# The last residual of a mixture of experts: normed rows stored and fetched, or taken again from x with a diagonal

## The chip, the cores and the metric

The kernel runs on one core of one Trainium2 chip. The metric is the device time of one execution in microseconds (us), smaller is better. Work is done by TensorE (PE, with its weight loads shown apart as PEld), VectorE (DVE), ScalarE (ACT) and GpSimd (POOL); SyncE (SP) issues nearly all DMA transfers. Each engine works through its own instructions strictly in order, and an instruction that waits holds up what stands behind it on that engine. All data is float32.

## The reference

Four sub-layers follow one another on `x`, eight sequences of 512 tokens with 256 channels (as the kernel groups them): differential attention, a two-layer local attention network, a pair of diffusion attentions, and a mixture of experts. Each is applied as `x + layernorm(f(layernorm(x)))`. The change touches the last one:

```
def _ln(x, g, b):
    mu = jnp.mean(x, axis=-1, keepdims=True)
    var = jnp.mean(jnp.square(x - mu), axis=-1, keepdims=True)
    return (x - mu) * jax.lax.rsqrt(var + EPS) * g + b
...
gates = jax.nn.softmax(xf @ gate_w, axis=-1)
topw, topi = jax.lax.top_k(gates, K)
topw = topw / jnp.sum(topw, axis=-1, keepdims=True)
combine = jnp.sum(topw[:, :, None] * jax.nn.one_hot(topi, E, dtype=xf.dtype), axis=1)
h = jnp.einsum('td,edh->teh', xf, w1) + b1
h = _ln(h, ln1_g, ln1_b)
h = jax.nn.gelu(h, approximate=False)
y = jnp.einsum('teh,ehd->ted', h, w2) + b2
out = jnp.einsum('ted,te->td', y, combine)
out = _ln(out + xf, ln_g, ln_b)
...
x = x + _layernorm(_L1_ffn_ref(_layernorm(x, axis=-1), ...), axis=-1)
```

Here `xf` is the already normed `x`: `(x - mean) * rs`, with `rs` the inverse standard deviation of the row. There are 8 experts, each token goes to 2 of them. `out + xf` goes through a layer norm over the 256 channels, and that norm subtracts the mean of each row.

## The kernel before

`x` stays in SBUF for the whole kernel as 128 partitions by 32 tiles by 256 channels: `self.xb(b)` is sequence b, `NT` = 4 tiles of 128 tokens. The time runs through four stages; the mixture of experts is spread over three places.

**The gate** (`gate`, L1238 on). For each sequence, while the diffusion stage still runs for the next one, it takes the moments of the rows (`moments`, which returns `mv`, mean and variance, and `rs`), makes the normed rows `xf` on DVE (`normed`, L194), stores them to DRAM (L1248, one buffer `self.xf[b]` for each sequence, made in `scratch`), and goes on to the gate matmul, the choice of two experts and their places. `self.vals[b]` holds for each of the two choices and four tiles the place and the weight. GpSimd then scatters the rows to the experts' places in DRAM (L1311). The last sequence's gate has no diffusion work left beside it.

**The expert loop** (`experts`). The scattered rows come in 72 tiles of 128 (`load`, L1380). `hidden` turns a tile, multiplies it with the first weights and norms the result; in that stretch of the kernel `self.logs` is off, so `power` (L172, L173) makes `rs` on GpSimd, with an exponent of -0.5 read from `mhalf`. `outer`, three tiles later, turns, applies GELU on ACT, multiplies with the second weights and scatters the results to `self.got` (L1413). In between, by `between()`, the program records `weights(b)` for sequences 0 to 3: for each choice k and tile t a 128x128 diagonal matrix `dw[b][:, k, t]`, the identity times the token weights as a per-partition scalar, on GpSimd (L1457). A scheduler puts the instructions into each engine's order when the program is built; the trace shows where they ended up.

**The finish** (`finish`, `scaled`). For each sequence it loads the normed rows (`xfb`, L1419) and the two results of each token (`egot`, L1422), and PE adds them up in PSUM (`pz`): identity times the normed rows, plus the diagonal of each choice times its results. `scaled` norms them: bn_stats and bn_aggr on DVE (L184, L186), `rs` as a logarithm and an exponential on ACT (L169, L170, `self.logs` on), `nm` = -mean x rs on DVE (L1443), and the scaling itself on ACT into `ez` (L1445). Then DVE multiplies by the scale of the norm (L1429), GpSimd adds its bias (L1430), a second `scaled` norms `ez` in place, GpSimd adds `x` (L1434) and SP stores the sequence (L1435). The tiles of the pool `e_fin` (`xfb`, `egot`, `ez`) have two buffers each, `pz` six buffers of half a sequence, `edw` four. For sequences 4 to 7 the diagonals are made here, on ACT (L1459), each set when the buffer of four sequences before is free.

Of the kernel before, what the change touches and what calls it, by code (L numbers as in the profile page):

```python
# [9 lines left out]
F32 = mybir.dt.float32  # L10
BF16 = mybir.dt.bfloat16
AF = mybir.ActivationFunctionType
ALU = mybir.AluOpType
AX = mybir.AxisListType
PSUM = bass.MemoryType.PSUM

P = 128
NB = 8
NT = 4
S = P * NT  # L20
D = 256
# [99 lines left out]
class Net:  # L121
# [6 lines left out]
    def begin(self, ctx):  # L128
        nc = self.nc
        keep = ctx.enter_context(self.tc.tile_pool(name="keep", bufs=1))  # L130
        self.const = keep.tile([P, C_N], F32, name="const", tag="const")
        nc.sync.dma_start(self.const, self.a["const"])
        self.ident = self.const[:, C_ID:C_ID + P]
        self.mhalf = keep.tile([P, 64], F32, name="mhalf", tag="mhalf")
        nc.gpsimd.memset(self.mhalf, -0.5)
        self.x = keep.tile([P, NB * NT, D], F32, name="x", tag="x")

        signs = keep.tile([1, TH], F32, name="signs", tag="signs")
        with nc.allow_non_contiguous_dma(reason="scales"):
            nc.sync.dma_start(signs, self.a["L1_attn_tau_t"].rearrange("h i j -> (i j) h"))  # L140
        nc.vector.tensor_single_scalar(signs, signs, 0.0, ALU.is_ge)
        flag = keep.tile([1, 1], F32, name="flag", tag="flag")
        nc.vector.tensor_reduce(flag, signs, AX.X, ALU.min)
        self.flag = keep.tile([1, 1], mybir.dt.int32, name="iflag", tag="iflag")
        nc.vector.tensor_copy(self.flag, flag)
        self.load_rows(range(1))
# [390 lines left out]
    def local(self, nb, early, first):  # L537
# [3 lines left out]
        with ExitStack() as ctx:  # L541
# [242 lines left out]
            for b in range(min(2, nb)):  # L784
                begin(b)
# [4 lines left out]
            for c in range(total + 1):  # L790
                if c + 1 < total:
                    r.add(rotated(c + 1))
                elif c < total:
                    r.add(prepared())
                for u, calls in enumerate(slots):
                    if c < total:
                        scores(c, u)
                    if u == 2 and c:
                        g.add(gated(c - 1))
                    half = (len(calls) + 1) // 2  # L800
                    for f in calls[:half]:
                        f()
                    before = (c, u - 1) if u else (c - 1, 7)
                    if before in weights:
                        turned(*before)
                    for f in calls[half:]:
                        f()
                    if before[1] % 2 and (before[0], before[1] // 2) in sums:
                        attend(before[0], before[1] // 2)
                    if u in (2, 6) and c + 2 < nb:  # L810
                        save(c + 2) if u == 2 else begin(c + 2)
                qkv.pop(c - 1, None)
# [370 lines left out]
    def scratch(self, ctx):  # L1183

        nc = self.nc
        dram = ctx.enter_context(self.tc.tile_pool(name="rows", bufs=1, space=bass.MemoryType.DRAM))
        self.rows = dram.tile([ROWS, D + 1], F32, name="xrows", tag="xrows")
        self.got = dram.tile([2 * NB * S + TILES * P, D], F32, name="yrows", tag="yrows")  # L1190
        self.xf = [dram.tile([P, NT, D], F32, name=f"xf{b}", tag=f"xf{b}") for b in range(NB)]

    def clear_rows(self, ctx):
        nc = self.nc
# [29 lines left out]
    def load_routes(self, ctx):  # L1224

        w = ctx.enter_context(self.tc.tile_pool(name="routes", bufs=1))
        self.gatew = w.tile([P, DC, NE], F32, name="gate", tag="gate")
        self.nc.sync.dma_start(self.gatew, self.a["L1_ffn_gate_w"].rearrange("(c p) f -> p c f", p=P))
        self.routes = w
        self.slots = [w.tile([P, 2 * NT], mybir.dt.int32, name=f"slots{b}", tag=f"slots{b}") for b in range(NB)]  # L1230
        self.vals = [w.tile([P, 2, 2, NT], F32, name=f"val{b}", tag=f"val{b}") for b in range(NB)]
        self.runs = [w.tile([P, NT + 1, NE], F32, name=f"run{b}", tag=f"run{b}") for b in range(NB)]
        self.table_ = w.tile([P, 4, TILES], mybir.dt.int32, name="table", tag="table")

# [3 lines left out]
    def gate(self, b, wk, small, ps):  # L1238

        nc, tc, row = self.nc, self.tc, self.row_of  # L1240
        tie = row(C_TIE, NE * NE).rearrange("p (e f) -> p e f", f=NE)
        tiles = lambda x: [x[:, t, :] for t in range(NT)]
        made = self.moments(small, tiles(self.xb(b)))
        yield
        both = wk.tile([P, 2, NT, D + 1], F32, name="xf", tag="xf")
        xf = both[:, 0, :, 0:D]
        self.normed(tiles(self.xb(b)), tiles(xf), *made)
        nc.sync.dma_start(self.xf[b], xf)  # L1248
        for k in range(2):
            nc.gpsimd.tensor_scalar_add(both[:, k, :, D], row(C_TOK, NT), float((k * NB + b) * S))  # L1250
        yield
# [45 lines left out]
        two = small.tile([P, 2, 2, NT, NE], F32, name="two", tag="two", bufs=2)  # L1297
# [1 line left out]
            for i, x in enumerate((pos, p)):  # L1299
                nc.vector.scalar_tensor_tensor(two[:, i, k], rank, float(k), x, ALU.is_equal, ALU.mult)  # L1300
        val, slots = self.vals[b], self.slots[b]
        nc.vector.tensor_reduce(val, two, AX.X, ALU.add)
        nc.vector.tensor_copy(slots, val[:, 0].rearrange("p k t -> p (k t)"))
        den = small.tile([P, NT], F32, name="den", tag="den")
        nc.vector.tensor_add(den, val[:, 1, 0, :], val[:, 1, 1, :])
# [49 lines left out]
    def experts(self, nb, rest):  # L1355
# [5 lines left out]
        with ExitStack() as ctx:  # L1361
# [4 lines left out]
            nc, tc, g = self.nc, self.tc, self.ew  # L1366
# [48 lines left out]
                tc.add_to_no_dep_group("store", i.ins)  # L1415

            def finish(b):
                xf = fin.tile([P, NT, D], F32, name="xfb", tag="xfb")
                nc.sync.dma_start(xf, self.xf[b])  # L1419
                both = fin.tile([P, 2, NT, D], F32, name="egot", tag="egot")  # L1420
                for k in range(2):
                    nc.sync.dma_start(both[:, k], results[:, k, b])  # L1422

                z = fin.tile([P, NT, D], F32, name="ez", tag="ez")
                pz = [psf.tile([P, 2, D], F32, name="pz", tag="psf") for t in range(0, NT, 2)]
                for t in range(NT):
                    self.mm(pz[t // 2][:, t % 2], [(self.ident, xf[:, t, :])] + [(dw[b][:, k, t], both[:, k, t, :]) for k in range(2)])
                scaled([pz[t // 2][:, t % 2] for t in range(NT)], [z[:, t, :] for t in range(NT)])
                nc.vector.tensor_mul(z, z, g["lg"].unsqueeze(1).to_broadcast([P, NT, D]))  # L1429
                nc.gpsimd.tensor_add(z, z, g["lb"].unsqueeze(1).to_broadcast([P, NT, D]))  # L1430
                yield
                each = [z[:, t, :] for t in range(NT)]
                scaled(each, each)
                nc.gpsimd.tensor_add(z, z, self.xb(b))  # L1434
                nc.sync.dma_start(xout[:, b], z)  # L1435
                yield

            def scaled(srcs, outs):

                n = len(srcs)  # L1440
                mv, rs = self.moments(few, srcs)
                nm = few.tile([P, n], F32, name="nm", tag="fnm")
                nc.vector.scalar_tensor_tensor(nm, mv[:, :, 0], -1.0, rs, ALU.mult, ALU.mult)  # L1443
                for i, (x, o) in enumerate(zip(srcs, outs)):
                    nc.scalar.activation(o, x, AF.Identity, bias=nm[:, i:i + 1], scale=rs[:, i:i + 1])  # L1445

            fin, few = (ctx.enter_context(tc.tile_pool(name=k, bufs=b, side="right")) for k, b in (("e_fin", 2), ("e_few", 3)))
            dw = {}

            def weights(b):  # L1450

                dw[b] = few.tile([P, 2, NT, P], F32, name="edw", tag="edw", bufs=4)
                for k in range(2):
                    for t in range(NT):
                        w = self.vals[b][:, 1, k, t:t + 1]
                        if b < 4:
                            nc.gpsimd.tensor_scalar_mul(dw[b][:, k, t], self.ident, w)  # L1457
                        else:
                            nc.scalar.mul(dw[b][:, k, t], self.ident, w)  # L1459
                        yield  # L1460

            between = Between()
            for b in range(min(4, nb)):
                between.add(weights(b))
            loaded, made = {}, {}
# [15 lines left out]
            for b in range(nb + 1):  # L1481
                if b < nb:
                    parts[b] = finish(b)
                    next(parts[b])
                if b + 4 < nb:
                    between.add(weights(b + 4))
                    between.end()
                if b:
                    next(parts.pop(b - 1))
# [68 lines left out]
```

## Time and profile before

| what | value |
|---|---|
| runs of the kernel | 3848.53, 3854.63, 3860.05 us (median 3854.63) |
| the profiled execution | 3837.43 us, of which the span is 3835.7 us |
| PE busy | 3484.9 us (91%) |
| DVE, ACT, POOL busy | 2201.1 (57%), 1855.1 (48%), 1583.6 us (41%) |
| mean granted TensorE clock | 0.953 |
| stores of normed rows (L1248) | 8 of 512 KB, issued from 2792.1 to 3348.3 us |
| loads of normed rows (L1419) | 8 of 512 KB, the first two at 3423.9 us, the last at 3785.3 us |
| diagonals on POOL (L1457) | 32, median 593 ns, from 3372.8 us |
| diagonals on ACT (L1459) | 32, median 401 ns, 3752.9 to 3777.5 us |
| expert loop | first tile load issued at 3372.8 us, first `egot` load issued at 3742.8 us |
| finish | from there to the end of the span, 92.9 us |

In the timeline lines that follow, the columns are start and length in us, engine, line of the kernel, operation, the tile written and those read, the shapes and the count, and in brackets how long the engine was idle before and what released it. The windows view gives busy time, granted clock and DMA traffic for a stretch.

### The profile page before, as it was taken

What the parts mean: (1) busy time and instruction counts of PE and PEld (TensorE: products, weight loads), DVE (VectorE), ACT (ScalarE), POOL (GpSimd) and SP (SyncE); (2) the same over time, 40 slices, a digit from 0 to 9 for tenths busy, and PEclk for the clock granted to TensorE, in tenths of its full rate; (3) what the DMA queues carried; (4) which work ended last, traced back from release to release, by engine and by line L of the source; (5) the groups of instructions that cost most, each with busy time, mean ns of one, the idle gap of its engine ahead of it and who ended that gap; (6) DMA issues with size and microseconds to landing.
All of it is one profiled execution on the core that took longest, in us unless ns stands there. A gap on an engine that the chain in (4) does not pass through costs nothing. (4 is left out here: it accounts for less than half of the span.)

```text
span 3835.7 us, 53567 instructions
## 1 busy us (share of the span) xinstructions
PE 3484.9 (91%) x20034; PEld 1894.1 (49%) x20034; DVE 2201.1 (57%) x4364; ACT 1855.1 (48%) x3719; POOL 1583.6 (41%) x1432
## 2 busy tenths in 40 slices
PE   8999999999987999999999999997988889679985
PEld 3344444444434566665665555564444444446554
DVE  6777777677646666665555666663244443344445
ACT  3555555555543444444444444443655555223334
POOL 3666766676654433333333343321012211153334
PEclk8999999999979999999999999998999999789997
DMA  9300000000001000000010000000000000421115
GB/s 350 119 1 7 6 7 1 7 7 1 6 6 34 3 4 4 4 4 25 4 34 9 9 9 9 9 20 23 1 23 23 23 17 17 147 68 55 53 43 167
DMA packets 95138, 130.29 MB, mean 34 GB/s; under 512 B 24702, under 2 KB 73242, under 8 KB 94874
## 3 DMA queue, kind: packets, MB, share of 16 engines
q1 hardware_dynamic: 88346, 108.94, 8.8%
q0 software_dynamic: 6528, 17.87, 1.3%
q8 instruction: 162, 2.65, 0.3%
q14 instruction: 102, 0.84, 0.1%
HBM read 57.40 MB, written 65.18 MB: 32 GB/s over the span
## 5 line engine op out<-in xcount | busy, mean ns | idle before, releaser
L372 ACT ACTIVATE e<-sa 128x1024 f32<-128x1024 f32 (+3 forms) x512 | 359.4, 702 | 303.7 <-PE sa L365 299.3
L393 POOL TENSOR_TENSOR e<-e,e 128x1536 f32<-128x1536 f32 (+2 forms) x192 | 451.7, 2353 | 91.4 <-PE po L388 81.4
L365 PE MATMUL sa<-qT,kT 32*128 32x512 f32 (+3 forms) x2048 | 431.9, 498 | 9.2 <-ACT e L372 8.8
L369 DVE TENSOR_REDUCE spread<-sc 128x2 f32<-128x256 f32 (+3 forms) x512 | 422.2, 825 | 15.3
L355 PE MATMUL sc<-kT,qT 32*128 32x128 f32 (+3 forms) x2048 | 421.6, 493 | 7.9 <-DVE spread L369 4.5
L656 ACT ACTIVATE lp<-lp,lnm 128x256 f32<-128x256 f32 (+1 forms) x512 | 240.1, 470 | 260.4 <-DVE lnm L648 156.0
L660 POOL TENSOR_TENSOR lp<-lp,lrs 128x1024 f32<-128x1024 f32 x64 | 121.1, 1893 | 529.0 <-DVE lrs L657 508.9
L368 DVE TENSOR_TENSOR sc<-sc,const 128x256 f32<-128x256 f32 x512 | 218.6, 427 | 173.7 <-PE sa L365 140.7
L1088 ACT ACTIVATE te<-tsa 128x1024 f32<-128x1024 f32 x256 | 248.9, 1023 | 135.8 <-PE tsa L1084 88.7
L355 PEld LDWEIGHTS sc<-kT,qT 32*128 32x128 f32 x2048 | 160.7, 189 | 284.9 <-DVE spread L369 113.1
L213 PE MATMUL lpa<-ghT,lw 128*128 128x512 f32 x640 | 284.8, 600 | 12.1 <-ACT ghT L569 12.1
L213 PE MATMUL lqk<-qkv,lhT 128*128 128x512 f32 x512 | 247.7, 622 | 2.3 <-DVE qk L607 1.6
L608 POOL TENSOR_TENSOR qk<-qk,over 128x1024 f32<-128x1024 f32 x64 | 151.4, 2366 | 207.8 <-DVE qk L607 207.8
L375 POOL TENSOR_SCALAR_AFFINE_SELECT e<-e 128x512 f32<-128x512 f32 x256 | 160.5, 640 | 177.0 <-ACT e L372 176.6
L1407 ACT ACTIVATE ehT<-eht,enorm 128x128 f32<-128x128 f32 x288 | 108.3, 457 | 208.6 <-PE eht L1403 207.7
L213 PEld LDWEIGHTS lpa<-ghT,lw 128*128 128x128 f32 x640 | 119.3, 190 | 163.3 <-issue 136.3
L388 PE MATMUL po<-e,v 128*32 128x512 f32 (+3 forms) x2048 | 188.3, 451 | 4.0 <-POOL e L375 3.6
L365 PEld LDWEIGHTS sa<-qT,kT 32*128 32x128 f32 x2048 | 160.9, 190 | 56.4 <-ACT e L372 29.7
L645 DVE TENSOR_TENSOR lp<-lsc,const 128x768 f32<-128x768 f32 (+1 forms) x128 | 138.6, 1083 | 86.5 <-PE lsc L642 85.9
L642 PE MATMUL lsc<-lkT,lqT 64*128 64x256 f32 (+1 forms) x1024 | 156.9, 386 | 28.1 <-DVE qk L607 28.0
L1084 PE MATMUL tsa<-tqT,tkT 32*128 32x512 f32 x1024 | 170.2, 673 | 5.9 <-DVE tqT L1039 3.3
L213 PE MATMUL py<-ew,ehT 128*128 x576 | 145.3, 397 | 23.5 <-ACT ehT L1407 23.5
(294 smaller groups left out, 6811.7 us busy)
## 6 DMA issues: line engine op xcount, KB each, us to landing
xrows<-zero SPq DMA_DIRECT2D x66, 514.0 KB
ex<-xrows SPq DMA_DIRECT2D x72, 128.5 KB
ew<-in_L_ffn_w_dram SPq DMA_DIRECT2D x16, 512.0 KB
egot<-yrows SPq DMA_DIRECT2D x16, 512.0 KB
x<-in_L_attn_X_dram SPq DMA_DIRECT2D x8, 512.0 KB
saved<-x SPq DMA_DIRECT2D x8, 512.0 KB
lx<-saved SPq DMA_DIRECT2D x8, 512.0 KB
xf<-xf SPq DMA_DIRECT2D x8, 512.0 KB
```

Source lines behind the costliest of these rows:

```text
L213: self.nc.tensor.matmul(out, lhsT=l, rhs=r, start=i == 0, stop=i == len(pairs) - 1)
L355: nc.tensor.matmul(sc[:, i, :w], lhsT=qT[g, self.tok(t)], rhs=kT[g, :w], start=True, stop=True)
L365: nc.tensor.matmul(sa[:, i, :S - k * P], lhsT=kT[g, self.tok(k)], rhs=qT[g, k * P:], start=True, stop=True)
L368: nc.vector.tensor_add(sc[:, :, w - P:w], sc[:, :, w - P:w], own)
L369: nc.vector.tensor_reduce(self.spread[n % 2][:, t, g0:g0 + 2, 0 if n % 2 else 16], sc[:, :, :w], AX.X, ALU.max, negate=True)
L372: nc.scalar.activation(x[:, h0:h0 + 2, :], sa[:, :, :S - k * P], AF.Exp, scale=0.25)
L375: nc.gpsimd.affine_select(x[:, :, :P], x[:, :, :P], [[0, 4], [1, P]], ALU.is_ge, 0.0, base=0, channel_multiplier=-1)
L388: nc.tensor.matmul(pos[n][group(g), k * P:], lhsT=seqs[b][1][:, k, 4 * r + g, :], rhs=x[:, g, :], start=k == 0, stop=k == 2)
L393: nc.gpsimd.tensor_add(y, y, es.pop((n, k)))
L656: nc.scalar.activation(x, x, AF.Exp, bias=nm[:, i, k:k + 1], accum_out=rs[:, i, k:k + 1])
L1084: m = nc.tensor.matmul(sa[i // 2][:, i % 2, :], lhsT=kT[q, self.tok(k)], rhs=qT[q, :], start=True, stop=True)
L1088: nc.scalar.activation(e[:, 2 * i:2 * i + 2, :], sa[i], AF.Exp)
```

## The change

The normed rows are no longer stored in the gate nor loaded in the finish. In the gate the inverse deviations `rs` (128x4) are copied into a third row of `self.vals[b]`. `weights(b)` makes a third set of diagonals from them, `dw[b][:, 2, t]`, so twelve for each sequence in place of eight, at the same places in the program: GpSimd for sequences 0 to 3, ACT for 4 to 7. In the finish PE multiplies this diagonal with `x`, which is in SBUF, where it multiplied the identity with the loaded normed rows. That gives `x * rs` rather than `(x - mean) * rs`; the two differ by one number for each row, which the norm that follows subtracts. The matmuls are as many as before and of the same shapes. `mhalf` shrinks from 64 to 8 columns (no more are read); `edw` takes 8 KB more of each partition over its four buffers and `xfb` 8 KB less over its two.

```diff
-        self.mhalf = keep.tile([P, 64], F32, name="mhalf", tag="mhalf")
+        self.mhalf = keep.tile([P, 8], F32, name="mhalf", tag="mhalf")
...
-        self.xf = [dram.tile([P, NT, D], F32, name=f"xf{b}", tag=f"xf{b}") for b in range(NB)]
...
-        self.vals = [w.tile([P, 2, 2, NT], F32, name=f"val{b}", tag=f"val{b}") for b in range(NB)]
+        self.vals = [w.tile([P, 3, 2, NT], F32, name=f"val{b}", tag=f"val{b}") for b in range(NB)]
...
         self.normed(tiles(self.xb(b)), tiles(xf), *made)
-        nc.sync.dma_start(self.xf[b], xf)
+        nc.vector.tensor_copy(self.vals[b][:, 2, 0], made[1])
...
-        nc.vector.tensor_reduce(val, two, AX.X, ALU.add)
+        nc.vector.tensor_reduce(val[:, 0:2], two, AX.X, ALU.add)
...
             def finish(b):
-                xf = fin.tile([P, NT, D], F32, name="xfb", tag="xfb")
-                nc.sync.dma_start(xf, self.xf[b])
                 both = fin.tile([P, 2, NT, D], F32, name="egot", tag="egot")
...
-                    self.mm(pz[t // 2][:, t % 2], [(self.ident, xf[:, t, :])] + [(dw[b][:, k, t], both[:, k, t, :]) for k in range(2)])
+                    self.mm(pz[t // 2][:, t % 2], [(dw[b][:, 2, t], self.xb(b)[:, t, :])] + [(dw[b][:, k, t], both[:, k, t, :]) for k in range(2)])
...
-                dw[b] = few.tile([P, 2, NT, P], F32, name="edw", tag="edw", bufs=4)
-                for k in range(2):
+                dw[b] = few.tile([P, 3, NT, P], F32, name="edw", tag="edw", bufs=4)
+                for k in range(3):
                     for t in range(NT):
-                        w = self.vals[b][:, 1, k, t:t + 1]
+                        w = self.vals[b][:, 1 + k // 2, k % 2, t:t + 1]
```

## The prediction

> **What bounds the kernel now.** I read the page's engine shares first: PE is busy 91% of 3835.7 us, so off-path work in the long stages costs nothing. The change touches three places, and I read each in the timeline: the gate, the start of the expert loop, and the finish after it.
>
> Start of the expert loop, timeline (start, length, engine, line, idle before and its releaser):
> ```profile
> 3372.80 18.57 POOL L1457 TENSOR_SCALAR edw<-const,val 128x128 f32<-128x128 f32 x32 [1.78 <-DMA xrows<-xf,slots]
> ...
> 3384.04 0.17 DVE L186 BATCH_NORM_AGGREGATE mv<-st 128x2 f32<-128x6 f32 x1
> ...
> 3391.46 0.19 POOL L172 TENSOR_SCALAR rs<-mv 128x1 f32<-128x1 f32 x1
> 3391.73 0.57 POOL L173 TENSOR_TENSOR rs<-rs,mhalf 128x1 f32<-128x1 f32 x1
> 3392.34 0.55 DVE L194 TENSOR_SCALAR eh<-eh,mv,rs 128x512 f32<-128x512 f32 x1 [8.13 <-POOL rs L173]
> ...
> 3393.03 1.09 PE L1403 MATMUL eht<-const,eh 128*128 128x128 f32 x4 [5.31 <-DVE eh L194]
> ```
> The 32 diagonals of sequences 0 to 3 stand in POOL's queue ahead of the first tile's `rs`. That tile's moments are there at 3384.2, but POOL gets to `rs` at 3391.46; DVE waits 8.13 us and PE 5.31 us. POOL sets this start.
>
> The expert loop then runs at PE's pace: from 3410 to 3725 one tile takes 4.8 us, with PE's gaps only a few tenths (releasers "issue" or ACT).
>
> Finish, timeline:
> ```profile
> 3763.64 0.31 ACT L169 ACTIVATE rs<-mv,const 128x4 f32<-128x4 f32 x1
> ...
> 3764.93 0.16 DVE L1443 SCALAR_TENSOR_TENSOR nm<-mv,rs 128x4 f32<-128x4 f32 x1
> ...
> 3765.18 2.08 ACT L1445 ACTIVATE ez<-ez,nm,rs 128x256 f32<-128x256 f32 x4
> ...
> 3769.80 0.38 SPq L1435 DMA_DIRECT2D out_dram<-ez  x1
> ...
> 3773.36 1.93 ACT L1445 ACTIVATE ez<-pz,nm,rs 128x256 f32<-128x256 f32 x4 [0.80 <-DMA out_dram<-ez]
> ...
> 3790.71 2.34 POOL L1434 TENSOR_TENSOR ez<-ez,x 128x1024 f32<-128x1024 f32 x1 [3.07 <-ACT ez L1445]
> ...
> 3791.02 2.04 DVE L1443 SCALAR_TENSOR_TENSOR nm<-mv,rs 128x4 f32<-128x4 f32 x1 [1.68 <-ACT rs L170]
> ...
> 3792.99 1.93 ACT L1445 ACTIVATE ez<-pz,nm,rs 128x256 f32<-128x256 f32 x4 [1.99 <-DMA out_dram<-ez]
> ```
> and its waits (waiter, releaser: us, times, longest):
> ```profile
> PE pz L213 <- DMA egot<-yrows: 9.5, 6, 4.6
> ACT ez L1445 <- DMA out_dram<-ez: 7.7, 5, 3.0
> PE pz L213 <- DMA xfb<-xf: 0.2, 1, 0.2
> ```
> `ez` has two buffers, so sequence b+2 is scaled only when the store of b has landed: scalings of sequences 0, 2, 4, 6 start at 3755.0, 3773.36, 3792.99, 3811.64. That ring (ACT, DVE, POOL, ACT, POOL, store) sets the end. Nearly nothing waits for `xfb`, the load that goes away (0.2 us). Also to be seen: an `nm` that takes 0.16 us alone takes 2.04 when issued beside a POOL tensor_tensor; it ends when POOL's does.
>
> **Part 1, the gate: 0.2 us.** Eight 512 KB stores leave SP's queue. Behind them stand the expert weights (from 3298.21). In the built program their first load also waits on PE and ACT, and it starts in the middle of the last diffusion work, 19.7 us after the seventh store was issued (3278.5), so it does not move. Added are 8 `val` copies of 128x4 on DVE, 0.16 us each by the cast of 128x8 at L1303. Seven lie in a stage where PE is 9 tenths busy and DVE 4 to 6; the eighth stands ahead of DVE's `xT` copy, which had been idle 1.31 us waiting for PE. Cover gone, they cost 8 x 0.16 = 1.3; I take 0.2. Gain bound: 0.
>
> **Part 2, start of the expert loop: +9.3 us.** In the built program the 48 POOL diagonals again stand in one block before the first `rs`, behind the same scatter. One costs 18.57/32 = 0.580 us; 16 more are 9.3. POOL was already last there, so all of it reaches DVE and PE, and the loop behind is PE's, so nothing is won back. The cover for the first 32 (12 us of first tiles, 3372.8 to 3384.2) is used up. What is not in the trace is a restart of PE after 15 us idle instead of 6. The windows by stretch show a granted clock of 0.52 from 3393 to 3402, then 1.00. Bounds: no more than now (0), or that whole slow stretch once more, 9 x 0.48 = +4.3. I take 0, being nearest to the row, where a gap of 6 us already led to about half speed.
>
> The Trainium skill ("TensorE: Matmul & The Clock Gate", the two-state table of its clock gate section) says the gate knows just two states, cold after about 3.4 us without work and warm after about 3.4 us of work. By it a longer gap costs nothing more; its warm-up is shorter than the 9 us here, and the trace decides. The sum by the rule is the one I take; by the other reading of the row it would be 4.3 us higher.
>
> **Part 3, the finish: +5.0 us.** Removed: six `xfb` loads (two of the eight had been issued at 3423.9). PE's matmul count is the same. Added: 16 ACT diagonals, at 0.306 us each (eight in a row took 2.45), and new places in the queues. I walked the built order with durations of this trace (scaling 1.93, multiply 1.22, POOL add 2.35, four bn_stats 1.4, norm 2.07, store landing 3.5 beside loads and 3.0 alone), on before's clock:
> - Up to 3763.64 nothing differs: ACT still does eight diagonals between the first scaling and the next `rs`.
> - Sequence 0: ACT now does 7 diagonals before `rs` (2.1 us), and on DVE `nm` stands behind a bn_stats of sequence 1's `ez`, which needs POOL's add (done about 3767.6). `nm` at 3768.05 instead of 3764.93, norm 3768.25 instead of 3765.18, store 3772.8 instead of 3769.80, scaling of sequence 2 at 3776.3 instead of 3773.36.
> - Sequence 1: ten diagonals (3.1) stand before its `rs` (3773.3 instead of 3769.22), and its norm is split around the scaling of 2: store 3781.7 instead of 3775.08 (+6.6).
> - Sequence 2: POOL's queue holds its add of the bias behind sequence 1's add of x, 3781.7 instead of 3776.68; store 3794.4 instead of 3787.67 (+6.7).
> - Sequence 3: an `nm` of sequence 4 comes between its bn_stats, beside POOL's add, and costs 2 us as in the line shown: norm 3796.8 instead of 3788.49 (+8.3), the largest delay.
> - Back: before, the store of sequence 2 took 5.3 us (3787.67 to 3792.99) beside `xfb` and `egot`; now the loads are over by then and 3.0 serve. Sequence 4 is scaled at 3798.8 (behind the norm of 3) instead of 3792.99 (+5.8), normed at 3808.25 instead of 3803.48, sequence 6 scaled at 3816.6 instead of 3811.64: +5.0, and from there the chain is the same.
>
> Bounds: -7.7, if every wait of ACT on a store went with the loads; +8.3, if the largest delay is not won back.
>
> **Sum:** 0.2 + 9.3 + 5.0 = 14.5. The profiled execution takes 3837.43 us (span 3835.7 and 1.7 around it), so 3851.9 with the change. The median shown, 3854.63, lies 17.2 above that one; the same 14.5 go on it: **3869**.
>
> **Rivals.**
> - **The lighter queue decides the finish.** For: five waits of ACT on stores, DMA engines 75% busy at 243 GB/s from 3746 to 3800. Against: the ring has 16 us of engine work per pair without them. At its best -7.7 with the 9.3: 3856.
> - **The finish is paced by bytes, not by the ring (not slower).** Six loads of 0.524 MB at 243 GB/s are 2.16 us each, 12.9 together; from a gain of 9.5 it outweighs POOL's block: 14.5 - 5.0 - 12.9 = -3.4, 3851. Against: PE waited 0.2 us for `xfb` and the last 36 us ran at 58 GB/s; only `egot` (9.5) speaks for it, and the ring hides that.
> - **The loop wins POOL's delay back.** Then 5.2 stay: 3860. Against: PE, in order, has no gaps to make up 9 us.
> - **The change makes a longer cold start** (4.3) and the delay of sequence 3 stays: 0.2 + 9.3 + 4.3 + 8.3 = 22.1: 3877.
>
> **How the numbers follow.** This kernel's measurement can tell 0.3% (11.6 us) from no change: faster is below 3843, slower above 3866. Forecast 0.58, lighter queue 0.18, bytes 0.08, won back 0.06, longer cold start 0.10. The forecast itself, with ring orders a few us either way and runs spread 3848.53 to 3860.05, lies above 3866 about 9 times in 10 and otherwise within (0.53 and 0.05); the cold start is slower (0.10); the other three within, but for 0.04 of bytes with a larger gain. Slower 0.63, same 0.33, faster 0.04. The range takes the second end from the lighter queue, the upper from the cold start, a little more for the spread: 3857 to 3878; the likeliest alone 3863 to 3876.
>
> **What would show it.** POOL's block `edw` 48 long and 27.9 us, ended near 3400.6; DVE's wait for the first `rs` 17.4 instead of 8.13; the expert loop to its last `py` as long as now. In the finish: no `xfb`, ACT's `edw` 48 times, ACT waiting less than 7.7 for stores, and from the first `egot` landing to the end 94 us instead of 89. Wrong if POOL's `rs` comes ahead of the diagonals, if the loop shortens, or if the finish is under 89 us.

## The result and the profile after

| | before | changed |
|---|---|---|
| median of the runs compared, us | 3844.26 (22 runs) | 3857.59 (22 runs) |
| spread of the runs, us | 3827.14 to 3862.93 | 3848.86 to 3874.76 |
| profiled execution, us (its span) | 3837.43 (3835.7) | 3857.06 (3855.3) |
| mean granted clock | 0.953 | 0.952 |
| start: first `ex` load issued to first `rs` of the loop on POOL | 18.7 | 27.9 |
| loop: from there to the first `egot` load issued | 351.4 | 352.1 |
| finish: from there to the end of the span | 92.9 | 97.6 |

The ratio is 1.0036, with a 95% interval of 1.0022 to 1.005: slower, by 13.8 us on 3844 (8 to 19). The three stages that the change touches grew by 9.2, 0.7 and 4.7 us, 14.6 together. The two profiled spans differ by 19.6; the other 5 us lie in the diffusion stage ahead of the first `ex` load (3372.8 before, 3377.8 after). That moment lay between 3341 and 3388 us in the profiles of this study, whatever had been edited, so a difference of 5 between two of them says nothing. For the same reason all that follows goes by these three lengths, and by ratios against runs of the kernel before on the same chip.

Timeline of the changed kernel at the start of the expert loop (columns as before):
```profile
3377.75 27.83 POOL L1456 TENSOR_SCALAR edw<-const,val 128x128 f32<-128x128 f32 x48 [1.70 <-DMA xrows<-xf,slots]
...
3389.11 0.17 DVE L186 BATCH_NORM_AGGREGATE mv<-st 128x2 f32<-128x6 f32 x1
...
3405.66 0.19 POOL L172 TENSOR_SCALAR rs<-mv 128x1 f32<-128x1 f32 x1
3405.93 0.57 POOL L173 TENSOR_TENSOR rs<-rs,mhalf 128x1 f32<-128x1 f32 x1
3406.54 0.55 DVE L194 TENSOR_SCALAR eh<-eh,mv,rs 128x512 f32<-128x512 f32 x1 [17.26 <-POOL rs L173]
...
3407.23 1.09 PE L1403 MATMUL eht<-const,eh 128*128 128x128 f32 x4 [14.44 <-DVE eh L194]
```
The block is 48 diagonals and 27.83 us long. The first moments are there at 3389.3, `rs` comes at 3405.66, and DVE waits 17.26 us for it instead of 8.13, PE 14.44 instead of 5.31.

Windows around the restart of PE, first of the kernel before (PE starts again at 3393.03), then of the changed kernel (3407.23):
```profile
3394.89:3398.31 3.42, 2.49 (x8) 2.25 (x9) 2.23 (x5) 2.40 (x8) 0.94 (x3) 0.50 0.12 38
3398.31:3401.72 3.41, 3.41 (x7) 2.03 (x7) 1.80 (x5) 0.14 (x1) 0.74 (x2) 0.50 0.00 0
3401.72:3405.13 3.41, 3.41 (x18) 2.54 (x16) 1.94 (x5) 0.29 (x1) 1.07 (x1) 1.00 0.11 38
...
3406.99:3410.41 3.42, 1.91 (x8) 1.56 (x9) 2.46 (x7) 1.76 (x5) 0.75 (x2) 0.50 0.14 38
3410.41:3413.82 3.41, 3.41 (x11) 2.85 (x10) 2.08 (x6) 1.50 (x4) 0.93 (x3) 0.50 0.00 0
3413.82:3417.23 3.41, 3.41 (x13) 2.23 (x12) 2.08 (x4) 0.00 (x0) 1.62 (x2) 1.00 0.00 0
```
The second number behind the stretch is PE's busy time, the third from the end the granted clock. The clock is back at 1.00 at 3401.72 in the kernel before, 8.7 us after the restart, and at 3413.82 in the changed kernel, 6.6 us after it: the longer idle time brought no longer slow stretch.

The finish of the changed kernel, timeline (`ez<-pz` is the first scaling of a sequence, `ez<-ez` the scaling of its second norm):
```profile
3770.20 1.93 ACT L1444 ACTIVATE ez<-pz,nm,rs 128x256 f32<-128x256 f32 x4
...
3778.85 2.15 ACT L1458 ACTIVATE edw<-const,val 128x128 f32<-128x128 f32 x7
3780.89 0.48 ACT L169 ACTIVATE rs<-mv,const 128x4 f32<-128x4 f32 x2
...
3783.30 2.08 ACT L1444 ACTIVATE ez<-ez,nm,rs 128x256 f32<-128x256 f32 x4 [1.15 <-DVE nm L1442]
3785.28 3.01 ACT L1458 ACTIVATE edw<-const,val 128x128 f32<-128x128 f32 x10
...
3789.06 1.09 ACT L1444 ACTIVATE ez<-ez,nm,rs 128x256 f32<-128x256 f32 x2
3791.32 1.93 ACT L1444 ACTIVATE ez<-pz,nm,rs 128x256 f32<-128x256 f32 x4 [1.17 <-DMA out_dram<-ez]
3793.13 1.09 ACT L1444 ACTIVATE ez<-ez,nm,rs 128x256 f32<-128x256 f32 x2
```
and its waits (waiter, releaser: us, times, longest):
```profile
ACT rs L169 <- DVE mv L186: 12.4, 5, 5.0
...
ACT ez L1444 <- DMA out_dram<-ez: 7.8, 3, 3.3
...
PE pz L213 <- DMA egot<-yrows: 3.7, 1, 3.7
```
Seven and ten diagonals stand in ACT's queue ahead of the second norms of sequences 0 and 1. The second norm of sequence 0 (3783.30) then starts 13.1 us behind its first scaling (3770.20), where before it was 10.2 (3755.0 to 3765.18). The second norm of sequence 1 is cut in two by the scaling of sequence 2. PE waits less for loads (3.7 us instead of 9.5), but ACT waits as long for stores as before (7.8 and 7.7).

### The profile page after: what moved, and what is told of

The parts are those of the page before. It is cut to its first block, busy times and chain, and to the rows that moved or that the text cites. A ratio compares the mean times of both kernels' runs of the same rounds, so it can differ in the third digit from the quotient of the medians.

```text
span 3855.3 us, 53566 instructions
## 1 busy us (share of the span) xinstructions
PE 3488.2 (90%) x20034; PEld 1898.8 (49%) x20034; DVE 2205.1 (57%) x4372; ACT 1859.0 (48%) x3735; POOL 1592.8 (41%) x1448
```

## The experiments

Every kernel was run beside the kernel before on the same chip. The median of the kernel before lay between 3811.62 and 3844.26 us in these comparisons, so a time is set only against the one measured with it. The stage lengths come from one profile of each, in us:

| kernel | start | loop | finish | ratio to the kernel before (95%) |
|---|---|---|---|---|
| before | 18.7 | 351.4 | 92.9 | |
| changed | 27.9 | 352.1 | 97.6 | 1.0036 (1.0022 to 1.005) |
| e1 before, 16 more diagonals on POOL | 28.0 | 351.4 | 92.9 | 1.0026 (1.0013 to 1.004) |
| e2 changed, no third diagonals | 18.6 | 353.4 | 94.2 | 1.0014 (0.9996 to 1.0032) |
| e3 before, 16 more diagonals on ACT | 18.7 | 354.7 | 101.3 | 1.002 (1.0007 to 1.0033) |
| e4 changed, POOL's diagonals on DVE | 11.3 | 354.7 | 97.7 | 0.999 (0.9975 to 1.0005) |
| e5 deviation folded into the gate weights | 11.2 | 354.8 | 93.9 | 0.9995 (0.9981 to 1.0008) |
| e6 = e5, 12 `eto`, order of ACT's diagonals | 10.7 | 336.6 | 94.7 | 0.9936 (0.992 to 0.9952) |
| e7 before, 12 `eto` | 18.7 | 336.9 | 93.0 | 0.9939 (0.9922 to 0.9955) |
| e9 changed, each copy 16 times | 27.9 | 351.2 | 97.6 | 1.006 (1.0043 to 1.0078) |
| e10 = e6, four `ez` | 10.8 | 336.4 | 83.1 | 0.9911 (0.9896 to 0.9925) |
| e11 changed, order of ACT's diagonals | 28.0 | 355.6 | 88.8 | 1.0016 (1.0005 to 1.0027) |
| e12 before, 12 `eto`, POOL's diagonals on DVE | 10.6 | 336.5 | 93.9 | 0.9941 (0.9929 to 0.9954) |
| e13 = e10, add of x on DVE | 10.8 | 336.5 | 84.9 | 0.9921 (0.9904 to 0.9938) |

Where nothing that concerns it was edited, a stage comes out alike within 1 us for start and finish (92.9, 92.9, 93.0; 97.6, 97.6, 97.7) and within 4.4 us for the loop with 6 buffers of `eto` (351.2 to 355.6).

**The changed kernel's added work alone, and its removed loads alone (e1, e2, e3).** e1 and e3 are the kernel before with the diagonals of its second result made twice, for sequences 0 to 3 (POOL) or 4 to 7 (ACT):
```diff
-                for k in range(2):
+                for k in ((0, 1, 1) if b < 4 else (0, 1)):
```
with the two tuples exchanged in e3. e2 is the changed kernel with `range(2)` and two sets in `edw`, and
```diff
-  [(dw[b][:, 2, t], self.xb(b)[:, t, :])] + ...
+  [(self.ident, self.xb(b)[:, t, :])] + ...
```
so it adds x itself and leaves out its factor, the inverse deviation.

> The kernel before, with the 16 diagonals of the second choice of sequences 0 to 3 made twice on POOL, nothing else. My theory: POOL's block is 48 x 0.58 = 27.9 us long, the first rs comes 28 us after the first tile load instead of 18.7, the expert loop is as long as before (351 us from the first rs to the first egot load) and the finish too (92.9), so +9.3 us, ratio 1.0024. Rival (the loop wins POOL's delay back): the same late start, a loop shorter by 6 to 9 us, total +0 to +3.

> The changed kernel without the third set of diagonals: PE multiplies the identity with x, so the factor rs is left out of the residual. Stores and loads are gone, the copies in the gate stay. My theory: first rs 18.7 us after the first tile load, finish 0 to 4 us shorter than 92.9, total 0 to -4 us against the kernel before. Rival (lighter queue): finish 85 us, total -8. Rival (bytes): finish 80 us, total -13. If the copies in the gate cost something, the first tile load comes 2 to 5 us late, as in the changed kernel.

> The kernel before, with the 16 diagonals of the second choice of sequences 4 to 7 made twice on ACT, nothing else. My theory: start and loop as before, finish 4 to 8 us longer than 92.9, since ACT is in the ring of ez and its rs and norms come late; total +4 to +8, ratio 1.001 to 1.002. Rival (ACT has room in the finish, the delay after the change is only POOL's): finish within 1 us of 92.9.

e1: the start is 28.0 as in the changed kernel, +9.3, and nothing else moved; the ratio, 1.0026, is 9.9 us. So the 16 POOL diagonals are the start's growth, and the loop gives none of it back. e2: without the loads and without the diagonals the start is back at 18.6 and the finish is 94.2. It is not shorter than before's 92.9, and far from the 80 to 85 of the theories in which bytes or the queue set it; removing the loads bought nothing. e3: 16 ACT diagonals more put 8.4 us on the finish while the loads are still there, a little above the 4 to 8 expected. In the changed kernel they stand at other places in ACT's queue and cost 3.4 beside e2 (94.2 to 97.6); the other 1.3 of its 4.7 is there without them, and little more than two profiles differ by.

**The same diagonals on another engine (e4).** The changed kernel with
```diff
-                            nc.gpsimd.tensor_scalar_mul(dw[b][:, k, t], self.ident, w)
+                            nc.vector.tensor_scalar_mul(dw[b][:, k, t], self.ident, w)
```
so 48 diagonals on DVE, which the built order spreads between the first tiles' work instead of one block.

> The changed kernel with the 48 diagonals of sequences 0 to 3 on DVE instead of POOL; the scheduler spreads them over the first 40 tiles. My theory: the first rs comes 12 to 13 us after the first tile load instead of 27.9, finish as after the change (97.5), so 12 to 16 us faster than the changed kernel, ratio to the kernel before 0.998 to 1.0005. Rival (what POOL gives back DVE loses in the loop): first rs as early, but the loop longer by up to 48 x 0.2 = 9.6 us, so only 5 us faster than the changed kernel, ratio 1.002.

Timeline of e4, start of the loop:
```profile
3358.71 0.69 PE L1388 MATMUL ext<-const,ex 128*128 128x128 f32 x2 [0.19 <-DMA ex<-xrows]
3358.77 0.28 DVE L1456 TENSOR_SCALAR edw<-const,val 128x128 f32<-128x128 f32 x1
...
3366.57 0.18 DVE L186 BATCH_NORM_AGGREGATE mv<-st 128x2 f32<-128x6 f32 x1
3366.99 0.19 POOL L172 TENSOR_SCALAR rs<-mv 128x1 f32<-128x1 f32 x1 [13.39 <-DVE mv L186]
```
POOL now has been idle for 13.39 us and waits for the moments, 0.24 us behind them. The start is 11.3, 16.6 less than in the changed kernel, and the ratio 0.0046 lower, 17.5 us. So moving POOL's block takes back what the change had cost, and perhaps more: of the 16.6 us of the start, 9.2 are the change's and 7.4 were lost in the kernel before too. The finish keeps its delay (97.7). Whether e4 beats the kernel before is not shown, as the interval of its ratio reaches from 0.9975 to 1.0005.

**The gate (e9).** The changed kernel with the copy into `val` made 16 times:
```diff
-        nc.vector.tensor_copy(self.vals[b][:, 2, 0], made[1])
+        for _ in range(16):
+            nc.vector.tensor_copy(self.vals[b][:, 2, 0], made[1])
```

> The changed kernel with the gate's copy of the inverse deviations made 16 times for each sequence: 8 x 15 more DVE copies of 128x4 of 0.16 us, 19 us of DVE work. It measures part 1, the cost of the copy in the gate. Theory (seven of eight copies are hidden beside PE's work in the diffusion stage, and DVE was idle 1.2 us ahead of xT at the last): at most 2.4 us more for the last sequence's 15 less the idle time, ratio to the changed kernel 1.000 to 1.001, so to the kernel before about 1.004. Rival (the copies lie on the path): 19 us more, ratio to the kernel before 1.0085; one copy would then cost 0.16 x 8 = 1.3.

The ratio is 0.0024 above the changed kernel's, 9 us for 120 copies of 0.16 (19.2 us): between the two theories, and the intervals (from 1.0043 and up to 1.005) overlap. Taken as it stands, the eight copies cost 8 x 9/120 = 0.6 us. The timeline of e9, last sequence, shows how the path is touched:
```profile
3363.00 1.59 DVE L1249 COPY val<-rs 128x4 f32<-128x4 f32 x8
3364.50 0.68 DVE L162 COPY xT<-pt 128x512 f32<-128x512 f32 x1
3365.10 0.57 DVE L1249 COPY val<-rs 128x4 f32<-128x4 f32 x3
```
Eight copies fill the time in which DVE waited for PE ahead of `xT`, three run in the wait behind it, and the rest stand between the gate's next instructions. From the start of `xf` to that of `rank` this sequence takes 9.89 us (3361.70 to 3371.59) instead of 9.76 in the changed kernel (3351.90 to 3361.66): the last sequence hardly pays for its copies. If the 9 us are real, they lie in the seven sequences ahead of it, beside the diffusion stage, and no stage length here can show them.

**Who paces the expert loop (e7).** Each tile's row of offsets `eto` has a ring of six buffers, and the scatter that reads the oldest must land before DVE writes it again. Timeline of the changed kernel in the middle of the loop:
```profile
3500.64 1.06 POOL L1413 DMA_INDIRECT yrows<-ey,eto  x1 [1.20 <-DVE ey L1412]
...
3503.17 0.16 DVE L1385 TENSOR_TENSOR eto<-ex,const 128x1 int32<-128x1 f32 x1 [1.49 <-DMA yrows<-ey,eto]
3503.24 0.17 DVE L186 BATCH_NORM_AGGREGATE mv<-st 128x2 f32<-128x6 f32 x1
...
3503.51 0.18 POOL L172 TENSOR_SCALAR rs<-mv 128x1 f32<-128x1 f32 x1 [1.82 <-DVE mv L186]
3503.78 0.57 POOL L173 TENSOR_TENSOR rs<-rs,mhalf 128x1 f32<-128x1 f32 x1
3504.39 0.55 DVE L194 TENSOR_SCALAR eh<-eh,mv,rs 128x512 f32<-128x512 f32 x1 [0.97 <-POOL rs L173]
3504.85 0.42 DVE L1412 TENSOR_TENSOR ey<-py,ebias 128x256 f32<-128x256 f32 x1
...
3505.55 1.06 POOL L1413 DMA_INDIRECT yrows<-ey,eto  x1 [1.20 <-DVE ey L1412]
```
DVE sits in front of `eto` until the scatter just issued has landed, 2.5 us after its start; behind `eto` in DVE's queue stand the moments, `eh` and `ey`, and behind `ey` the next scatter, 4.91 us after the last. The experiment changes one number in the kernel before:
```diff
-  to = small.tile([P, 1], mybir.dt.int32, name="eto", tag="eto", bufs=6)
+  to = small.tile([P, 1], mybir.dt.int32, name="eto", tag="eto", bufs=12)
```

> The kernel before with one edit: 12 instead of 6 buffers for the offset tile (eto) of the expert loop's scatter. It asks who paces the loop. Theory (the ring of eto: DVE waited 88.6 us in 57 waits for the scatter's landing): the loop from the first rs to the first load of the results takes 343 to 346 instead of 351.4; ratio 0.998. Rival (PE paces it, as the prediction said, and DVE's waits are only slack): loop 351, ratio 1.000. Rival (the next ring, the four buffers of ey, takes its place): 349 to 351, with DVE waiting for the scatter at ey instead.

DVE's waits from 3420 to 3720, kernel before:
```profile
DVE eto L1385 <- DMA yrows<-ey,eto: 87.1, 56, 3.1
DVE eh L194 <- POOL rs L173: 62.4, 61, 2.2
DVE eh L1396 <- PE ph L213: 1.4, 3, 0.6
```
and with twelve buffers (e7):
```profile
DVE eh L1396 <- PE ph L213: 70.7, 58, 1.3
DVE eh L194 <- POOL rs L173: 64.5, 63, 2.2
```
The wait for the scatter is gone, and one for PE's `ph` stands in its place: now PE sets the pace (busy 275.4 of these 300 us, with a wait of 0.40 us a tile for ACT's GELU). The scatters of e7 follow each other every 4.77 us by the median, instead of 4.90 before and 4.91 in the changed kernel. Behind the first dozen tiles the loops of these two have twelve and ten gaps of 5.0 to 6.7, most with a longer wait of DVE for a landing ahead of them (in the changed kernel's gap of 6.68 it is 3.25 us instead of 1.49); in e7 one gap of 6.28 is left after the first dozen tiles. The loop falls from 351.4 to 336.9, further than the 343 to 346 expected, and the ratio is 0.9939. PE, DVE and the ring of `ey` are ruled out as the pace of the loop before. The ratio says 23 us (17 to 30), more than the 14.5 that the loop lost; no stage shows the rest.

**The deviation without diagonals (e5, e6).** In e5 PE adds x with the identity, and the sum of gate probabilities is multiplied with the row's inverse deviation ahead of its reciprocal:
```diff
+        nc.vector.tensor_mul(den, den, made[1])
```
Each row of the sum then comes out multiplied by its own deviation, which the following norm takes out, so it computes what the change does, up to that norm's epsilon, with 64 diagonals as before; those of sequences 0 to 3 are on DVE. e6 adds the 12 buffers and puts `between.add(weights(b + 4))` behind `next(parts.pop(b - 1))`.

> The changed kernel without a third set of diagonals: PE adds x with the identity, and the gate's sum of the two probabilities is multiplied with the row's inverse deviation before its reciprocal, so each row of the sum comes out multiplied with its own deviation, which the norm behind it removes (up to its epsilon). The 32 diagonals of sequences 0 to 3 are made on DVE, between its other work. My theory: the start of the expert loop goes from 18.7 us (before) to 11 to 12, because no block stands ahead of the first rs on POOL; DVE's 32 diagonals at about 0.2 us lengthen the loop by 1 to 3; the finish takes about 94, as with the identity in e2. Together -3 to -8 us against the kernel before, ratio 0.998 to 0.999. Rival (the loads mattered after all, and were only hidden by the diagonals): finish 85 to 88, ratio 0.996. Rival (DVE's added work lands on the path of the loop): loop 358 or more, ratio 1.000 or above.

> The kernel of the run e5 with two more edits: 12 instead of 6 buffers for the offset tile of the expert loop's scatter (eto), and ACT's diagonals of sequence b+4 issued behind the second half of the norm of sequence b-1 instead of ahead of it. Theory (the loop is paced by the scatter that a buffer of eto waits for, 4.91 us a tile against 4.77 us of PE work; and the finish by ACT's queue): loop 343 to 346 instead of 351 to 355, finish 88 to 92 instead of 94; ratio 0.994 to 0.996 against the kernel before. Rival (PE or another ring sets the same pace): the loop stays at 351 or more and the ratio at that of e5.

e5: start 11.2 and finish 93.9 as expected, loop 354.8, just above the 352 to 354 expected; 0.9995 is at best half of the gain expected, and its interval holds both no gain and all of it. e6: the loop falls to 336.6 as in e7, and the ratio with it; its finish, 94.7 instead of the 88 to 92 expected, is not shortened by the order.

**The order on ACT's queue (e11).** The same move of `weights(b + 4)` in the changed kernel and nothing else.

> The changed kernel with one edit: ACT's diagonals of sequence b+4 are issued behind the second norm of sequence b-1 instead of ahead of it. In the built program six and ten diagonals no longer stand ahead of the second norms of sequences 0 and 1 in one piece, and the scalings are no longer split. Theory (the places of the 16 added diagonals in ACT's queue set the finish's +4.6): finish 92 to 95 instead of 97.5, ratio 1.0022 to 1.003. Rival (their number and DVE's and POOL's order set it, not their places): 97 to 98, ratio 1.0036.

Timeline of e11 around the second norms of sequences 0 and 1:
```profile
3763.43 1.93 ACT L1444 ACTIVATE ez<-pz,nm,rs 128x256 f32<-128x256 f32 x4
...
3772.66 1.28 ACT L1458 ACTIVATE edw<-const,val 128x128 f32<-128x128 f32 x4
3773.83 2.07 ACT L1444 ACTIVATE ez<-ez,nm,rs 128x256 f32<-128x256 f32 x4
...
3778.94 2.06 ACT L1444 ACTIVATE ez<-ez,nm,rs 128x256 f32<-128x256 f32 x4
3780.91 0.68 ACT L1458 ACTIVATE edw<-const,val 128x128 f32<-128x128 f32 x2
3781.82 1.94 ACT L1444 ACTIVATE ez<-pz,nm,rs 128x256 f32<-128x256 f32 x4 [0.23 <-DMA out_dram<-ez]
```
The second norm of sequence 0 (3773.83) starts 10.4 us after its first scaling (3763.43), where the kernel before had 10.2, no norm is split, and the finish is 88.8 with all 48 of ACT's diagonals, 8.7 less than in the changed kernel and 4 less than in the kernel before; 92 to 95 was expected. The ratio falls by 0.0020, though the two intervals still touch (up to 1.0027, from 1.0022). So 48 diagonals need not cost anything: it was their places that cost 4.7. In e6, with 32 diagonals, the same move gained nothing (93.9 to 94.7); why it does not gain there, and which order is best, these runs leave open.

**The freed space, and the kernel before with the other gains (e10, e12).** e10 is e6 with
```diff
-                z = fin.tile([P, NT, D], F32, name="ez", tag="ez")
+                z = fin.tile([P, NT, D], F32, name="ez", tag="ez", bufs=4)
```
which fits because `xfb` is gone and no third diagonals take its 8 KB. e12 is the kernel before with 12 `eto` buffers and POOL's 32 diagonals on DVE.

> The kernel of the run e6 (identity times x, 12 buffers of eto) with four buffers of ez in the finish instead of two: the 8 KB per partition that the two buffers of xfb took, and which no third set of diagonals takes here. Theory (the ring of ez sets the finish: a scaling waits for the store two sequences before): the finish goes from 94.7 to 80 to 88, and ratio 0.989 to 0.992 against the kernel before. Rival (the engines' work and the chain inside one sequence, ACT, DVE, POOL, ACT, POOL, set it, and the store's landing is only in front of other waits): 92 to 95, ratio 0.993 to 0.994 as in e6.

> The kernel before, loads of the normed rows and all, with two edits: the 32 diagonals of sequences 0 to 3 made on DVE, between its other work, instead of in a block on POOL, and 12 buffers of eto. It asks whether the gains of the runs before need the change at all. Theory (they do not): start 11 instead of 18.7, loop 337 to 340 (DVE's 32 diagonals cost little there), finish 93; ratio 0.992. Rival (with the loop at the pace of other engines DVE's diagonals land on its path): loop 343 or more, ratio 0.994 or above, so no better than eto alone.

e10's finish is 83.1 and no wait of ACT for a store is left among its waits: the ring of two `ez` buffers had set the finish, and with four of them the change at last pays. The kernel before has no room for four as it stands; no run made room there by other means. e12's stages are 10.6, 336.5 and 93.9; its ratio, 0.9941, does not show the 8 us of the start against e7's 0.9939, though the intervals (0.9929 to 0.9954, 0.9922 to 0.9955) leave room for it. Against the kernel before, e12's three stages are shorter by some 22 us together and its ratio says 23, so it is e7's ratio that is low for its stages. Between e12 and e10 the finish differs by 10.9 us, the ratio by 0.0030: that is what leaving out the loads is worth when its space goes to `ez`. e10 is the fastest version found, 0.9911 against the kernel before.

**The held instruction (e13).** e10 with the last add on DVE:
```diff
-                nc.gpsimd.tensor_add(z, z, self.xb(b))
+                nc.vector.tensor_add(z, z, self.xb(b))
```

> The kernel of the run e10 with one edit: the last add of the finish (x onto the normed z) is made on DVE instead of POOL. It tests the reading of DVE's nm, which takes 0.16 us alone and up to 2.04 beside a POOL tensor_tensor, ending with it. Theory (DVE's scalar_tensor_tensor is held while POOL runs a tensor_tensor of 2.35 us, and this stands in the finish's chain): half of these POOL instructions go, so nm is held less than half as often, DVE pays 1.22 a sequence for the add, and the finish goes from 83.1 to 76 to 81, ratio 0.9895 to 0.9905 against the kernel before. Rival (nm is not held by POOL, but the profile only shows it long while it waits for something else): nm keeps its long times, DVE's added 8 x 1.22 = 9.8 us make the finish as long or longer, 83 to 90, ratio 0.991 to 0.993.

All 16 `nm` now last 0.145 to 0.165 us, so the hold is real and goes with POOL's add. But the finish is 84.9, not 76 to 81, and the ratio 0.9921. In e10 five `nm` were held, 4.4 us together, while DVE's eight added instructions take 1.21 us each, 9.7 together; and POOL's other add now waits for DVE, 32.5 us in six waits from 3725 to 3770.

## Why the prediction was right, step by step

The sum was 14.5 and the three stages grew by 14.6; the ratio predicted by it, 14.5 on 3837.43, is 1.0038 against 1.0036 measured. That the sums meet within a tenth is luck: 0.7 of the 14.6 is the loop's, less than the 4.4 by which loops differ that nobody edited, part 1's 0.2 lies outside the three stages, and the finish came out 0.3 lower. The two large terms are right for the reasons given. The predicted time, 3869, is 11 us above the 3857.59 measured, nearly all of it because it was put on a median of three runs, 3854.63, while the runs of the kernel before in the comparison have 3844.26. The time measured lay 0.6 us above the lower end of the range and outside the part called likeliest, 3863 to 3876: that it lay in the range at all is luck too. By the mark set there for slower, above 3866, it would not count as slower; the ratio, whose interval starts at 1.0022, shows that it is.

- **Part 1, the gate, 0.2.** Small as said; e9 makes it some 0.6, with an uncertainty as large, and no stage shows it. No run shows the 0.2 itself.
- **Part 2, the start, +9.3.** Right: +9.2 in the changed kernel, +9.3 in e1, and gone in e2 and e4. The block is 27.83 us long, against 27.9 predicted, and DVE's wait 17.26 against 17.4. No longer cold start followed: the clock was back 6.6 us after PE's restart instead of 8.7. The bound of +4.3 fell, and the reading taken there (a longer gap costs nothing more) agrees. The 9 us that the prediction held against a warm-up of about 3.4 us do not speak against it: 5.3 of the 8.7 passed with PE busy in part, and the clock came back behind the first 3.41 us that PE filled.
- **"The expert loop then runs at PE's pace."** This step was wrong. The pace was the landing of the scatter that a buffer of `eto` waits for; e7 shows it. PE's gaps of a few tenths were read off as nothing, but 4.90 - 4.77 = 0.13 us a tile are such gaps, and the waits view of that stretch had the cause, 87.1 us of DVE's waits for this transfer. (In the changed kernel the chain of waits on the page has it as its largest entry, 4% of the span.) The conclusion, that the loop neither lengthens nor wins POOL's delay back, held all the same (351.4, 352.1; e1 351.4): a ring that paces a loop has no slack either.
- **Part 3, the finish, +5.0.** Measured +4.7. The walk's times can be laid on the changed kernel's, 15.2 us earlier (its first scaling starts at 3770.20 instead of 3755.0): norm of sequence 0 at 3768.1 (predicted 3768.25), scaling of 2 at 3776.1 (3776.3), store of 1 at 3781.6 (3781.7), store of 2 at 3794.1 (3794.4), norm of 3 at 3796.2 (3796.8), scaling of 4 at 3798.2 (3798.8), scaling of 6 at 3815.9 (3816.6). By the end the walk is 0.7 too late, and by this clock the finish grew by 4.4; another 0.3 lies ahead of the first scaling, which starts 12.4 us after the first `egot` load instead of 12.2. That the places of the diagonals cost it is shown by e11, and that the ring of `ez` sets the finish by e10. Not met: ACT's waits for stores stayed at 7.8 in place of falling below 7.7, three long ones instead of five.
- **The rivals.** Lighter queue and bytes needed a finish of 80 to 85; e2 has 94.2. Won back: e1 gives nothing back. Longer cold start: the slow stretch behind the restart is 6.6 us, 8.7 before.

## What to carry to other kernels

A transfer that hardly anybody waits for (0.2 us here) is worth nothing when it goes. The instructions that replace it are paid in full where they stand in a queue ahead of the first instruction of a chain: 16 of them on POOL cost 9.2 us. So look at what stands behind new instructions in the queue of the engine that makes them, and move them, to another place or another engine, before judging the change. The gain of such a change can be the space it frees; here 8 KB per partition paid 10.9 us in the finish as two more `ez` buffers, and nothing as a third set of diagonals. An engine that is busy nine tenths is not thereby the pace: find the small wait that comes back every period, and see whether a ring of buffers closes it.

## What the runs showed of the hardware

The loop's indirect scatter of 128 rows lands 2.5 us after its start by the median in the traces that hold its landings, but now and then later: up to 3.1 us in e13, 4.0 in e2 and 4.6 in e3. A wait that stands in front of every tile's work takes each late landing in full; with twelve buffers none is waited for. The steady pitch alone, 72 x 0.13, is 9 us of the 14.5 that twelve buffers gave; the rest fits the late landings, but was not taken apart.

In all traces of this study the granted clock is 0.5 or 1.0, and it changes on a grid of 3.41 us. Eight runs have PE idle ahead of the first `rs`: the kernel before, e2, e3 and e7 for 5.3 to 5.5 us, the changed kernel, e1, e9 and e11 for 13 to 15. Behind the restart the clock was back after 5.1 to 8.7 us in the first four and after 5.9 to 6.6 in the others. It came back each time behind a stretch of the grid in which PE was busy 81 to 100%, and stayed at 0.5 behind the stretch ahead of that one, with 44 to 73%. By these eight, how soon PE fills such a stretch decides, and not how long it was idle.

A 128x4 `scalar_tensor_tensor` on DVE of 0.16 us was held for up to 2.31 us (in the changed kernel) beside POOL `tensor_tensor` instructions of 2.35 to 2.41. Timelines of e10, POOL and then DVE:
```profile
3759.20 2.35 POOL L1433 TENSOR_TENSOR ez<-ez,x 128x1024 f32<-128x1024 f32 x1
...
3759.28 0.75 DVE L184 BATCH_NORM_STATS2 st<-ez 128x6 f32<-128x256 f32 x2 [2.46 <-POOL ez L1429]
3759.95 1.63 DVE L1442 SCALAR_TENSOR_TENSOR nm<-mv,rs 128x4 f32<-128x4 f32 x1
3761.50 0.74 DVE L184 BATCH_NORM_STATS2 st<-ez 128x6 f32<-128x256 f32 x2
```
The bn_stats beside the same POOL instruction runs in its usual time; `nm`, which reads two tiles, ends at 3761.58, 0.03 behind POOL's end at 3761.55. The Trainium skill ("SBUF — State Buffer", section "SBUF: two separate sides") says that DVE and GpSimd share a pair of ports as an exclusive lock for the whole instruction, which a DVE instruction with two inputs in SBUF needs; this case agrees: in the kernels before and changed and in e10, each `nm` that starts while either of POOL's adds runs ends within 0.05 us of it, and all others last 0.13 to 0.17 us; and e13, where the add went to DVE, leaves no `nm` over 0.165 us.
